# Five edits in a four-layer vision kernel: exp table load, norm shifts, leaky relu, sums of exp, skip loads

## The chip, the cores and the metric

The kernel runs on one core of a Trainium2 chip. The metric is the device time of one execution in microseconds (us). A core has five engines, each with an instruction queue of its own that is worked off in order: TensorE (PE, matmuls; its weight loads are listed as PEld), VectorE (DVE), ScalarE (ACT), GpSimd (POOL) and SyncE (SP, which here only issues DMAs). Engines wait for each other through semaphores.

## The reference

Four layers follow each other on `x[4, 64, 64, 128]` in float32. Layer 0 is a selective scan, layer 1 attention over all 4096 tokens of an image, layer 2 a convolution block, layer 3 attention in a 7 x 7 neighbourhood with an MLP. What the edits touch is this:

```
# layer 0
xn = _ln(input, ln1_w, ln1_b)                       # mean and variance over 128 channels
...
h = exp(d_t[..., None] * A) * h + (d_t * x_t)[..., None] * B_t     # 4096 steps, 4 directions
ys = ... + Ds * xs                                   # the skip term
...
h2 = gelu(_ln(x, ln2_w, ln2_b) @ fc1_w + fc1_b) @ fc2_w + fc2_b
# layer 1
scores = einsum('bnd,bmd->bnm', f, g)
beta = softmax(scores, axis=1)
att = einsum('bnc,bnm->bcm', hv, beta)
# layer 2, end
xc = _bn(concatenate([x1, x2]), bn_cat)
xc = where(xc >= 0, xc, 0.1 * xc)
# layer 3
attention(_ln(x)), then x + mlp(_ln(x)) with gelu
```

## The kernel before

**Stages.** `network` (L1611) first makes the inputs of image 0's scan (`scan_inputs`, L275). Then `selective_scan` (L451) runs for the images 0 to 3, one after the other, and beside each scan the other work of the images is put: beside image 0's scan the scan inputs of images 1 to 3, beside the scan of image i the stages of image i - 1 (`rest`, L1579: `scan_output`, `layer1`, `layer2`, `layer3_attention`). The MLP of layer 3 of an image runs within the `scan_output` of the next one. For image 3 nothing is left to put beside it: its stages run alone at the end with `wide` true (larger tiles, since the scan's buffers are free), and last comes `layer3_mlp_alone`.

**Order.** The order of each engine's queue is laid down when the program is built, by a scheduler that simulates the program's time and takes, of the instructions that are ready, the one with the smallest priority number. The scan is traced with a large number (`SCAN_FIRST`), the activations of a group and the table load after it with a very small one (-100 * `SCAN_FIRST`), the rest in order of tracing. So an edit can also shift instructions around it.

**The scan.** One unit covers 64 of 256 channels, 4 of 16 states and 512 steps: a product `dB` on POOL (L498, 128x1024), two exponentials `dA` on ACT (L504, 128x512 into PSUM, three buffers), two scans on DVE (L506), two products with C (L511 on DVE, or one L519 on POOL for 5 or 7 units of 16), and a copy of the last state on ACT (L513, L515). `total` (L527) adds up with PE (L553) into `py`; with `j == 0` it first loads a tile `y_before` (three buffers) and adds it to `py`: for direction 0 the skip term, read from `xc` in four DMAs of 32 partitions (L535), for directions 2 and 3 the sums of earlier directions (L540, L544). These loads share SP's queue with those of `dt`, `du` (L481) and `bc` (L489).

**Table loads.** ACT has one table of functions active at a time; exp and ln are in one, gelu and silu in others. `Together` (L101) collects the gelu or silu activations of a chunk, makes all of them wait for the group's last matmul, and then calls `exp_table` (L95), which loads the table with exp and ln. That load depends on the group's last activation by a dependency of the kind `Sync`. Where the program has an activation whose function isn't in the active table, a load is put ahead of it when the program is built, and the profile shows it under that activation's line.

**Norms.** `layernorm_T` (L179) takes 4 x 128 tokens: statistics on DVE (L188, L190), rstd on ACT as exp(-0.5 ln(var + eps)) (L175, L176), the shift -mean * rstd for the four tiles on DVE (L192, 128x4), four scaled copies on ACT (L196), four transposes on PE (L199) and one activation (L200). It is called 128 times: 32 chunks each in `scan_tokens`, `scan_output`, `layer3_attention` and `layer3_mlp`.

**Layer 1.** For each of 8 chunks of 512 columns and 8 steps t: four score matmuls (L783), exp on ACT (L787, one instruction of 128x2048 when `wide`), four matmuls with the values into `pa` (L831), and four with ones into `den` (L839), which gives the sums of exp. The scores of step t + 1 are traced ahead of the products of step t. A float32 matmul is two instructions in the profile, so a group of four counts 8.

**Layer 2, end.** For each of 8 chunks (L965): normalisation from PSUM into `t` on ACT (L973), max(0.1 t, t) on DVE (L974), a matmul with `cv4` (L981), and the last activation (L983, L984).

Of the kernel before, what the change touches and what calls it, by code (L numbers as in the profile page):

```python
# [27 lines left out]
F32 = mybir.dt.float32  # L28
AF = mybir.ActivationFunctionType
ALU = mybir.AluOpType  # L30
# [11 lines left out]
LC = 512  # L42
NCH = NT // LC
RC = LC // W
# [27 lines left out]
def span(c, n=LC):  # L72
    return slice(c * n, (c + 1) * n)
# [9 lines left out]
    tc.cur_priority = kept  # L83


def after(tc, later, earlier):
    tc.add_manual_dep(
        later.ins,
        earlier.ins.name,
        mybir.DependencyInfo(mybir.DependencyClass.Sync, mybir.DependencyReason.DATA),  # L90
        reason="group",
    )


def exp_table(tc, K, done):  # L95

    with priority(tc, K, -100 * SCAN_FIRST):
        after(tc, tc.nc.scalar.preload_act_table_set("natural_log_exp_and_others"), done)


class Together:  # L101
# [77 lines left out]
def layernorm_T(tc, K, pool, psum, x, w, b, out):  # L179


    nc = tc.nc
    stats = pool.tile([128, 4, 6], F32, name="ln_stats", bufs=2)
    mv = pool.tile([128, 4, 2], F32, name="ln_mv", bufs=2)
    rstd = pool.tile([128, 4], F32, name="ln_rstd", bufs=2)
    shift = pool.tile([128, 4], F32, name="ln_shift", bufs=2)
    for t in range(4):
        nc.vector.bn_stats(stats[:, t, :], x[:, t, :])  # L188
    for t in range(4):
        nc.vector.bn_aggr(mv[:, t, :], stats[:, t, :])  # L190
    rstd_of(nc, K, rstd, mv[:, :, 1])
    nc.vector.scalar_tensor_tensor(shift, mv[:, :, 0], -1.0, rstd, ALU.mult, ALU.mult)  # L192
    xn = pool.tile([128, 4, 128], F32, name="ln_xn", bufs=1)
    pt = psum.tile([128, 4, 128], F32, name="ps")
    for t in range(4):
        nc.scalar.activation(  # L196
            xn[:, t, :], x[:, t, :], AF.Identity, bias=shift[:, t : t + 1], scale=rstd[:, t : t + 1]
        )
        nc.tensor.transpose(pt[:, t, :], xn[:, t, :], K.ident)  # L199
    nc.scalar.activation(out, pt.rearrange("p t c -> p (t c)"), AF.Identity, bias=b, scale=w)  # L200
# [250 lines left out]
def selective_scan(tc, K, S, D, img):  # L451
# [8 lines left out]
    nc = tc.nc  # L460
    pool, psum = S.pool, S.psum
# [6 lines left out]
    for k in ORDER:  # L468
# [4 lines left out]
        for i in range(NCH):  # L473
            c = NCH - 1 - i if back else i
            for hf in range(2):
                dts, dus = [], []
                for pp in range(2):
                    rows = span(2 * hf + pp, 32)
                    for name, src, out in (("dt", D.delta, dts), ("du", D.du, dus)):
                        t = pool.tile([128, 2, LC], F32, name=name, bufs=4)  # L480
# [6 lines left out]
                for j in range(NJS):  # L487
# [6 lines left out]
                    hcs, made = [], []  # L494
# [32 lines left out]
                    def total(k=k, c=c, hf=hf, j=j, hcs=hcs, made=made, py=py):  # L527
                        if j == 0:
                            py.append(psum.tile([128, LC], F32, name="py"))
                            before = pool.tile([128, LC], F32, name="y_before", bufs=3)  # L530
                            if k == 0:
                                for pp in range(2):
                                    for g in range(2):
                                        q = 2 * pp + g
                                        nc.sync.dma_start(  # L535
                                            before[32 * q : 32 * q + 32, :], D.xc[img][c][span(2 * hf + pp, 32), g, :]
                                        )
                                nc.tensor.matmul(py[0], S.skip[:, hf, :], before, start=True, stop=False)
                            elif k >= 2:
                                nc.sync.dma_start(before, D.y_first[img][k % 2][c][:, hf, :])  # L540
                                nc.tensor.matmul(py[0], K.ident, before, start=True, stop=False)
                            if k == 2:
                                cols = pool.tile([128, NCH, RC, RC], F32, name="y_before", bufs=3)
                                nc.sync.dma_start(  # L544
                                    cols.rearrange("p c a b -> p c (a b)"),
                                    D.y_cols[img][:, :, c, hf].rearrange("c p x -> p c x"),
                                )
                                nc.tensor.matmul(
                                    py[0].rearrange("p (a c b) -> p a c b", a=RC, b=RC), K.ident,
                                    cols.rearrange("p c a b -> p a c b"), start=False, stop=False,  # L550
                                )
                        for q in range(4):
                            mm = nc.tensor.matmul(  # L553
                                py[0][32 * q : 32 * q + 32, :], S.pick, hcs[q // 2][:, q % 2, :],
                                start=(k == 1 and j == 0), stop=(j == NJS - 1),
                            )
                            if q == 0:
                                for m in made:
                                    after(tc, mm, m)
                        if j == NJS - 1:  # L560
                            y = pool.tile([128, LC], F32, name="y_sum")
                            if k == 3:
                                nc.scalar.copy(
                                    y.rearrange("p (b a) -> p b a", b=H), py[0].rearrange("p (a b) -> p b a", b=H)
                                )
                                nc.scalar.dma_start(
                                    D.y_cols[img][c][:, :, hf, :], y.rearrange("p (r x) -> p r x", r=NCH)
                                )
                            else:
                                nc.scalar.copy(y, py[0])  # L570
                                to = D.y[img][c] if k == 2 else D.y_first[img][k % 2][c]
                                nc.scalar.dma_start(to[:, hf, :], y)
# [145 lines left out]
def layer1(tc, K, A, D, img, xT, wide):  # L718
# [4 lines left out]
    nc = tc.nc  # L723
    NP = 4 if wide else 2
    with ExitStack() as ctx:
        big = ctx.enter_context(tc.tile_pool(name="l1_big", bufs=1))
        pool = ctx.enter_context(tc.tile_pool(name="l1", bufs=1))
        psum = ctx.enter_context(tc.tile_pool(name="l1_p", bufs=1, space=PSUM))
        load = loader(tc, big, A, 1)
# [47 lines left out]
        def scores(c, t):  # L777
            es = []
            for p in range(4 // NP):
                ps = pair(NP)  # L780
                for u in range(NP):
                    quad = span(NP * p + u, 32)
                    nc.tensor.matmul(  # L783
                        ps[:, u, :], f[quad, t // 4, span(t % 4, 128)], g[quad, c, :], start=True, stop=True
                    )
                e = pool.tile([128, NP, LC], F32, name="e", bufs=10 // NP)
                made = nc.scalar.activation(e, ps, AF.Exp)  # L787
                es += [e[:, u, :] for u in range(NP)]
            return es, made

        xT_view = xT.rearrange("c (p j) -> c j p", j=NJ)

# [29 lines left out]
        for c in range(NCH):  # L822
            pa = psum.tile([128, LC], F32, name="pa")
            den = None
            ready = scores(c, 0)
            for t in range(8):
                es, made = ready
                if t + 1 < 8:
                    ready = scores(c, t + 1)
                for q in range(4):  # L830
                    nc.tensor.matmul(  # L831
                        pa, v[:, 8 * q + t, :], es[q],
                        start=(t == 0 and q == 0), stop=(t == 7 and q == 3),
                    )
                if not K.general:
                    if den is None:
                        den = psum.tile([128, LC], F32, name="den")
                    for q in range(4):
                        mm = nc.tensor.matmul(  # L839
                            den[32 * q : 32 * q + 32, :], K.ones[:, :32], es[q],  # L840
                            start=(t == 0), stop=(t == 7),
                        )
                        if q == 0:
                            after(tc, mm, made)
                if c == 0 and t in (1, 3, 5) and not K.general:
                    keys((t + 1) // 2)
            finish(c, pa, den)
# [55 lines left out]
def layer2(tc, K, A, D, img, xT, wide):  # L903
# [3 lines left out]
    nc = tc.nc  # L907
    with ExitStack() as ctx:
        big = ctx.enter_context(tc.tile_pool(name="l2_big", bufs=1))
        pool = ctx.enter_context(tc.tile_pool(name="l2_w", bufs=2))  # L910
        psum = ctx.enter_context(tc.tile_pool(name="l2_ps", bufs=8 if wide else 4, space=PSUM))
        load = loader(tc, big, A, 2)
# [5 lines left out]
        norms = load("norms", [128, len(NORMS2), 4], D.w2_norms)  # L918
# [46 lines left out]
        for c in range(NCH):  # L965
# [5 lines left out]
            nc.tensor.matmul(ps[64:128, :], cv2p, xT[:, span(c)], start=True, stop=True)  # L971
            t = pool.tile([128, LC], F32, name="cat")
            nc.scalar.activation(t, ps, AF.Identity, bias=norms[:, 5, 1:2], scale=norms[:, 5, 0:1])  # L973
            nc.vector.scalar_tensor_tensor(t, t, 0.1, t, ALU.mult, ALU.max)  # L974
            po = psum.tile([128, 4, 128], F32, name="ps")
            nc.tensor.matmul(
                po.rearrange("p t c -> p (t c)"), K.ones[0:1, :], bias.rearrange("p t c -> p (t c)"),
# [768 lines left out]
```

## Time and profile before

| what | value |
|---|---|
| median of three runs | 9356.33 us (9351.10 to 9378.78) |
| profiled execution: time, span | 9352.68 us, 9350.9 us |
| instructions | 99598 |
| PE busy | 7472.2 us, 80% of the span |
| DVE busy | 7109.1 us, 76% |
| POOL busy | 7052.9 us, 75% |
| ACT busy | 5607.1 us, 60% |
| mean granted PE clock | 0.85 |

The page names a group of instructions by its line, engine and operation, then the tiles that it writes and reads with their shapes, the count, the busy time in us and the mean of one in ns, and after a second bar the time that the engine sat idle just before them and what ended it. In a list of waits a row reads "engine, line that waited <- what it waited for: us in total, times, longest". In a timeline a row begins with the start and the duration in us. In the page's second part each digit is the busy share of one fortieth of the span, in tenths.

### The profile page before, as it was taken

To read this page: it belongs to the slowest core of one execution; us is meant where nothing else is said; L and a number is where in the kernel's file an instruction comes from. 1 tells how busy PE (TensorE), PEld (TensorE's weight loads), DVE (VectorE), ACT (ScalarE), POOL (GpSimd) and SP (SyncE) were. 2 spreads that over 40 slices of the span, in tenths; PEclk is the share of its full clock that TensorE was granted. 3 is DMA by queue.
4 is the path that set the end of the run, shared out by engine and by line. 5 is a ranking of instruction groups with operands and counts; after the bars stand their busy time and mean duration, and the time that the engine had idled before them with its cause. 6 is when DMAs were issued, how large, how long until landed. Compare 5 with 4: busy or idle time off the path is not lost. (4 is left out here: it accounts for less than half of the span.)

```text
span 9350.9 us, 99598 instructions
## 1 busy us (share of the span) xinstructions
PE 7472.2 (80%) x30564; PEld 2808.5 (30%) x30564; DVE 7109.1 (76%) x8543; ACT 5607.1 (60%) x10676; POOL 7052.9 (75%) x3064
## 2 busy tenths in 40 slices
PE   8647768696779997787789988877799977788987
PEld 3112222231332232233322333333222322343333
DVE  0798787777889988988899989888999898820033
ACT  4646666665566666557766655567666555553345
POOL 1977988979789988987899979987999699800000
PEclk9658678686789998888899988888899888889988
DMA  2766766667544546565455555554455455510020
GB/s 101 262 216 214 250 216 222 248 208 271 183 154 169 176 155 210 175 209 173 142 173 178 178 180 178 190 196 151 160 179 175 152 198 176 196 40 3 1 82 28
DMA packets 720492, 1581.76 MB, mean 169 GB/s; under 512 B 207157, under 2 KB 332236, under 8 KB 715597
## 3 DMA queue, kind: packets, MB, share of 16 engines
q1 hardware_dynamic: 589645, 1399.12, 44.1%
q10 hardware_dynamic: 130304, 176.19, 5.3%
q8 instruction: 245, 4.01, 0.2%
q14 instruction: 298, 2.44, 0.1%
HBM read 1280.47 MB, written 283.59 MB: 167 GB/s over the span
## 5 line engine op out<-in xcount | busy, mean ns | idle before, releaser
L498 POOL TENSOR_TENSOR dB<-du,bc 128x1024 f32<-128x1024 f32 x2048 | 4806.9, 2378 | 699.3 <-DVE hc L506 229.0
L504 ACT ACTIVATE dA<-dt,w_A_log 128x512 f32<-128x512 f32 x4096 | 2782.1, 689 | 569.5 <-DVE hc L506 284.3
L506 DVE TENSOR_TENSOR_SCAN dA<-dA,state,dB 128x512 f32<-128x512 f32 x2128 | 2627.0, 1272 | 382.5 <-POOL dB L498 187.8
L519 POOL TENSOR_TENSOR hc<-hc,bc 128x1024 f32<-128x1024 f32 x832 | 1976.3, 2380 | 238.8 <-ACT state L515 131.1
L506 DVE TENSOR_TENSOR_SCAN hc<-dA,state,dB 128x512 f32<-128x512 f32 x1456 | 1800.6, 1267 | 279.4 <-ACT dA L504 133.8
L511 DVE TENSOR_TENSOR hc<-dA,bc 128x512 f32<-128x512 f32 x2432 | 1560.5, 675 | 91.7 <-PE py L553 82.4
L553 PE MATMUL py<-hc,pick 128*32 128x512 f32 x8192 | 1276.3, 699 | 316.7 <-POOL hc L519 208.3
L513 ACT COPY state<-dA 128x1 f32<-128x1 f32 x2128 | 327.7, 158 | 1349.5 <-DVE hc L511 1328.5
L831 PE MATMUL pa<-e,l_v 128*128 128x512 f32 x2048 | 1062.9, 649 | 5.1 <-ACT e L787 3.9
L787 ACT ACTIVATE e<-pair 128x1024 f32<-128x1024 f32 (+1 forms) x448 | 508.0, 1134 | 271.3 <-PE pair L783 268.6
L783 PE MATMUL pair<-l_g,l_f 32*128 32x512 f32 x2048 | 530.7, 668 | 168.1 <-ACT e L787 125.9
L831 PEld LDWEIGHTS pa<-e,l_v 128*128 128x128 f32 x2048 | 371.9, 199 | 661.6 <-issue 637.8
L553 PEld LDWEIGHTS py<-hc,pick 128*32 128x32 f32 x8192 | 217.2, 118 | 1093.0 <-issue 500.4
L1272 PE MATMUL pair<-table,ident 128*128 128x512 f32 x768 | 420.8, 674 | 115.1 <-ACT e L1282 90.9
L506 DVE TENSOR_TENSOR_SCAN dA<-dA,dB 128x512 f32<-128x512 f32 x304 | 357.7, 1212 | 200.2 <-POOL dB L498 166.5
L245 PE MATMUL ps<-band,w_conv_diag 128*128 128x504 f32 (+3 forms) x1152 | 493.1, 586 | 4.1 <-ACT band L314 3.4
L408 PE MATMUL ps<-xdbl,w_dt_w 9*128 9x512 f32 x512 | 351.0, 935 | 181.0 <-ACT delta L359 128.1
L416 POOL TENSOR_TENSOR du<-delta,xc 128x1024 f32<-128x1024 f32 x128 | 337.1, 2639 | 177.0 <-DMA bc_dram<-xdbl 160.5
L199 PE MATMUL ps<-ident,ln_xn 128*128 128x128 f32 x512 | 132.3, 356 | 356.3 <-ACT ln_xn L196 287.2
L1282 ACT ACTIVATE e<-pair 128x1024 f32<-128x1024 f32 (+1 forms) x224 | 254.2, 1135 | 153.4 <-PE pair L1276 153.0
L217 PE MATMUL ps<-xnT,w_fc_w 128*128 128x512 f32 x512 | 275.6, 672 | 66.8 <-ACT mlp_h L224 27.3
L231 PE MATMUL ps<-mlp_h,w_fc_w 128*128 128x512 f32 x512 | 283.5, 702 | 53.9 <-ACT mlp_h L224 53.9
(270 smaller groups left out, 8547.6 us busy)
## 6 DMA issues: line engine op xcount, KB each, us to landing
bc<-bc_dram SPq DMA_DIRECT2D x1024, 512.0 KB
dt<-delta_dram SPq DMA_DIRECT2D x512, 512.0 KB
du<-du_dram SPq DMA_DIRECT2D x512, 512.0 KB
delta_dram<-delta ACTq DMA_DIRECT2D x128, 512.0 KB
du_dram<-du SPq DMA_DIRECT2D x128, 512.0 KB
table<-biasT_dram SPq DMA_DIRECT2D x72, 512.0 KB
y_first_dram<-y_sum ACTq DMA_DIRECT2D x128, 256.0 KB
y_before<-y_first_dram SPq DMA_DIRECT2D x128, 256.0 KB
```

The source lines that it names most:

```text
L245: mm = nc.tensor.matmul(out[:, r0 - row0 : r1 - row0, c0:c1], lhsT((dy + 1) * 3 + dx + 1), src[:, r0 + dy : r1 + dy, c0 + dx : c1 + dx], s ...
L408: nc.tensor.matmul(pd[:, d, :], dt_w[rows, o, d * 128 : (d + 1) * 128], xdbl[rows, i, :], start=True, stop=True,)
L498: nc.gpsimd.tensor_mul(dB, dus[pp], mid(bct[:, 0, :], 2))
L504: nc.scalar.activation(dA, dts[pp][:, g, :], AF.Exp, scale=S.A[:, k, j, pr, g : g + 1])
L506: nc.vector.tensor_tensor_scan(hg[:, order], dA[:, order], dB[:, g, order], 0.0 if i == 0 else state[:, j, pr, g : g + 1], ALU.mult, ALU.add,)
L511: mm = nc.vector.tensor_mul(hc[:, g, :], dA, bct[:, 1, :])
L519: made.append(nc.gpsimd.tensor_mul(hc, hc, mid(bct[:, 1, :], 2)))
L553: mm = nc.tensor.matmul(py[0][32 * q : 32 * q + 32, :], S.pick, hcs[q // 2][:, q % 2, :], start=(k == 1 and j == 0), stop=(j == NJS - 1),)
L783: nc.tensor.matmul(ps[:, u, :], f[quad, t // 4, span(t % 4, 128)], g[quad, c, :], start=True, stop=True)
L787: made = nc.scalar.activation(e, ps, AF.Exp)
L831: nc.tensor.matmul(pa, v[:, 8 * q + t, :], es[q], start=(t == 0 and q == 0), stop=(t == 7 and q == 3),)
L1272: nc.tensor.matmul(ps[:, u, :], K.ident, t[:, u, :], start=True, stop=False)
```

## The change

1. `after` takes a kind of dependency, and the exp table's load now hangs on the group's last activation by `NoSync`: the order stays, without a semaphore between them.
2. `layernorm_T` makes the shift on ACT: -rstd once for the four tiles (`less`), then four activations of one column each, mean times `less`. The instruction L192 on DVE is gone.
3. `y_before` has four buffers in place of three, and the skip term is loaded in two DMAs of 64 partitions in place of four of 32.
4. In `wide` layer 1 (image 3 only), DVE adds the tiles of exp over the eight steps of a chunk in `total` (a copy at t = 0, adds after), and only at t = 7 four matmuls with ones make `den` of it.
5. At the end of layer 2 a second activation writes the normalised value into PSUM in place, and the maximum on DVE reads it there, in place of reading `t` twice.

```diff
-def after(tc, later, earlier):
+def after(tc, later, earlier, kind=mybir.DependencyClass.Sync):
     tc.add_manual_dep(
-        later.ins,
-        earlier.ins.name,
-        mybir.DependencyInfo(mybir.DependencyClass.Sync, mybir.DependencyReason.DATA),
-        reason="group",
+        later.ins, earlier.ins.name, mybir.DependencyInfo(kind, mybir.DependencyReason.DATA), reason="group"
     )
...
     with priority(tc, K, -100 * SCAN_FIRST):
-        after(tc, tc.nc.scalar.preload_act_table_set("natural_log_exp_and_others"), done)
+        load = tc.nc.scalar.preload_act_table_set("natural_log_exp_and_others")
+        after(tc, load, done, mybir.DependencyClass.NoSync)
...
+    less = pool.tile([128, 4], F32, name="ln_less", bufs=2)
     shift = pool.tile([128, 4], F32, name="ln_shift", bufs=2)
...
-    nc.vector.scalar_tensor_tensor(shift, mv[:, :, 0], -1.0, rstd, ALU.mult, ALU.mult)
+    nc.scalar.activation(less, rstd, AF.Copy, scale=-1.0)
+    for t in range(4):
+        nc.scalar.activation(shift[:, t : t + 1], mv[:, t, 0:1], AF.Copy, scale=less[:, t : t + 1])
...
-                            before = pool.tile([128, LC], F32, name="y_before", bufs=3)
+                            before = pool.tile([128, LC], F32, name="y_before", bufs=4)
                             if k == 0:
                                 for pp in range(2):
-                                    for g in range(2):
-                                        q = 2 * pp + g
-                                        nc.sync.dma_start(
-                                            before[32 * q : 32 * q + 32, :], D.xc[img][c][span(2 * hf + pp, 32), g, :]
-                                        )
+                                    nc.sync.dma_start(
+                                        before[span(pp, 64), :],
+                                        D.xc[img][c][span(2 * hf + pp, 32)].rearrange("d g t -> g d t"),
+                                    )
...
-                                cols = pool.tile([128, NCH, RC, RC], F32, name="y_before", bufs=3)
+                                cols = pool.tile([128, NCH, RC, RC], F32, name="y_before", bufs=4)
...
-            return es, made
+            return es, made, e
...
-                es, made = ready
+                es, made, e4 = ready
...
-                if not K.general:
+                if wide:
+                    if t == 0:
+                        total = pool.tile([128, NP, LC], F32, name="total", bufs=2)
+                        nc.vector.tensor_copy(total, e4)
+                    else:
+                        nc.vector.tensor_add(total, total, e4)
+                    if t == 7:
+                        es, made = [total[:, q, :] for q in range(4)], None
+                if not K.general and (t == 7 or not wide):
                     if den is None:
                         den = psum.tile([128, LC], F32, name="den")
                     for q in range(4):
                         mm = nc.tensor.matmul(
                             den[32 * q : 32 * q + 32, :], K.ones[:, :32], es[q],
-                            start=(t == 0), stop=(t == 7),
+                            start=(t == 0 or wide), stop=(t == 7),
                         )
-                        if q == 0:
+                        if q == 0 and made is not None:
                             after(tc, mm, made)
...
-            nc.vector.scalar_tensor_tensor(t, t, 0.1, t, ALU.mult, ALU.max)
+            nc.scalar.activation(ps, ps, AF.Identity, bias=norms[:, 5, 1:2], scale=norms[:, 5, 0:1])
+            nc.vector.scalar_tensor_tensor(t, t, 0.1, ps, ALU.mult, ALU.max)
```

## The prediction

> **What bounds the kernel now.** I read the page's slices first, then the waits of the stretch in which the scan runs (222 to 8205 us), then the rows of the edited lines, then timelines.
>
> ```profile
> PE   8647768696779997787789988877799977788987
> DVE  0798787777889988988899989888999898820033
> ACT  4646666665566666557766655567666555553345
> POOL 1977988979789988987899979987999699800000
> ```
>
> One digit is 233.8 us. GpSimd (POOL) and VectorE (DVE) are at eight or nine tenths until slice 35; then POOL has nothing left and PE carries the last 1146 us alone. So there are two regimes, and each edit is priced in the one it falls in. In the scan's 7983 us POOL is busy 7016.1, DVE 6888.7, ScalarE (ACT) 5001.4. POOL's work is untouched by the diff, so only its 967 us of idle time can shrink. What ended that idle time:
>
> ```profile
> POOL dB L498 <- DVE hc L506: 229.0, 72, 21.4
> POOL dB L498 <- DMA bc<-bc_dram: 200.0, 86, 11.5
> POOL hc L519 <- ACT state L515: 131.1, 61, 6.5
> POOL dB L498 <- DVE dA L506: 101.4, 39, 7.5
> POOL hc L519 <- DVE hc L506: 78.4, 25, 13.7
> ```
>
> (us in total, times, longest.) Three of these five rows are DVE: 408.8 us. It lies where norms run beside the scan: from 4200 to 4600 us POOL is busy 313.5 of 400, while from 7000 to 7200 it has no gap at all.
>
> ```profile
> L192 DVE SCALAR_TENSOR_TENSOR ln_shift<-ln_mv,ln_rstd 128x4 f32<-128x4 f32 x128 | 113.1, 894 | 71.9 <-ACT ln_rstd L176 71.4 <-ACT state L513 0.3
> L974 DVE SCALAR_TENSOR_TENSOR cat<-cat 128x512 f32<-128x512 f32 x32 | 38.0, 1187 | 9.9 <-ACT cat L973 9.9
> L98 ACT ACT_TABLE_LOAD x100 | 128.3, 1283 | 1.8
> L504 ACT ACT_TABLE_LOAD x44 | 56.5, 1283 | 0.8
> ```
>
> The norm's shift has four elements per partition and a mean of 894 ns. Its median is 164 ns and its longest 7483; after 8205 us, with POOL silent, 27 of them take 4.05 us (150 ns each). Something holds it while POOL works. The last row is the other oddity: an activation of the scan reloads the table 44 times, although L98 reloads it 100 times on purpose. A timeline of ACT shows why:
>
> ```profile
> 9257.26 2.42 ACT L224 ACTIVATE mlp_h<-ps,w_fc_b 128x512 f32<-128x512 f32 x4 [0.95 <-PE ps L217]
> 9259.70 1.28 ACT L175 ACT_TABLE_LOAD   x1
> 9261.00 0.30 ACT L175 ACTIVATE ln_rstd<-ln_mv,eps 128x4 f32<-128x4 f32 x1
> 9261.31 1.28 ACT L98 ACT_TABLE_LOAD   x1
> ```
>
> The planned load (L98) had been put behind another activation, which needed the same table and got a load of its own; the planned one then loads it a second time. L504 (44), L175 (12) and L176 (2) hold 58 such loads, 50 of them within the scan.
>
> Last, the last image's attention, PE alone:
>
> ```profile
> 8576.99 3.70 PE L831 MATMUL pa<-e,l_v 128*128 128x512 f32 x8
> 8580.62 1.07 PE L839 MATMUL den<-e,ones 128*32 128x512 f32 x8
> 8581.61 1.14 PE L783 MATMUL pair<-l_g,l_f 32*128 32x512 f32 x8
> 8582.68 3.70 PE L831 MATMUL pa<-e,l_v 128*128 128x512 f32 x8
> ```
>
> A step t lasts 5.69 us with no gap on PE: values 3.63, sums of exp 0.99, next scores 1.07 (start to start).
>
> **What the Trainium skill says.** "SBUF — State Buffer", section "SBUF: two separate sides": DVE and GpSimd share a port pair under an exclusive lock; a DVE instruction with two SBUF inputs waits for a whole GpSimd instruction that reads SBUF. The trace agrees: L192 and L974 have two SBUF inputs and stretch beside POOL; L984, same size as L974 with one PSUM input, has a mean of 671 ns. "ScalarE: Activation LUTs", section "What ACT_TABLE_LOAD costs": 1283 ns for a load, which every row here has, plus a drain of 1380, which this trace does not show (after the load at 9259.70 the next activation starts 0.02 us later). It also prices an activation at 186 ns + 0.833 per element + 93 per pointer operand, with 93 of overlap back to back; L196 (128 elements, two pointers) should be 479 and has a median of 482. "VectorE: DVE Perf Modes", its perf-mode tier table: an fp32 add of 2048 takes 2293 ns (L1284 here: 2292), an fp32 copy 1227.
>
> **Part 1, sums of exp on DVE (last image).** Of 8 x 8 groups of den matmuls, 7 x 8 = 56 go, 0.99 us each: **-55.6 us**, all of it on PE, which sets the end there. Added: per chunk one copy (1.23 us by the skill) and seven adds (2.29 us by L1284). The cover is the shortened step of 4.70 us; DVE is busy only 17.2 of 400 us between 8500 and 8900. The last add is ready 2.3 us after the last exp; den is asked for after another 3.63 us of values, so PE doesn't wait. If the adds took over 4.70 us the step would follow DVE. The e buffer (two) is released later by the add, but its next use is 4.7 us on. Behind an add in DVE's queue can stand the maximum L748, three times in the first chunk, for which PE already waits 3.9 us in all; up to 2.3 us each, I take +2. Sum **-54**.
>
> **Part 2, norm shift to ACT.** 128 norms. Removed from DVE: within the scan 93 instructions and 107.8 us (26.1 + 16.2 + 28.1 + 37.4 by stretch), DVE's head-of-queue wait for rstd there (15.4 us), and ACT's wait for the shift (79.2 us: 9.1, 15.8, 19.9, 34.4). Added to ACT per norm: five instructions. Floor: three one-element copies run in 0.26 us in this trace, so 0.45; ceiling: five times L175's 0.29 without overlap, 1.45. By the skill's formula 0.19 + 4 x 0.28 - 3 x 0.09 = 1.03 us, which I take: 96 us within the scan. Behind them in ACT's queue stand the scan's dA, for which DVE waits (363 us today).
>
> **Part 3, table load.** If each planned load directly follows its group, the 58 doubles go: 58 x 1.283 = 74.4 us of ACT, 64.2 within the scan. Removing the wait itself is worth nothing: 1.8 us idle before all 100. Bounds: 0 (the order stays) to 74.4; I take all of it as ACT time.
>
> **Part 4, leaky relu.** DVE within the scan: 24 x (1.352 - 0.671) = 16.3 us less. ACT: one more activation from PSUM with two pointers, 0.777 us by L973: 24 x 0.777 = 18.6 us within the scan. In the last image layer 2 is bound by PE (110.6 of 120 us), so eight more cost at most the last one, 0.8.
>
> **Part 5, skip term.** 128 issues fewer on SP at a median of 0.41 us: 53 us of a queue that mostly waits for buffers (1108 and 1064 us for bc buffers alone). Same bytes, same rows. The fourth y_before buffer lets these loads be queued earlier. Bounds: a gain up to part of the 200 us in which POOL waits for bc; a loss as in rival D. I take 0.
>
> **Sum.** Within the scan DVE gets back 107.8 + 15.4 + 16.3 = 139.5 us; ACT 64.2 + 79.2 - 96 - 18.6 = 29 us. What of that reaches the end? POOL waits for DVE in a share of the time only; where norms run, POOL stands for about 22% and DVE is at 85%, so DVE sets the pace there about half the time. I take 0.45 of 139.5 (63) and little of ACT's (2): **-65**, bounds 0 and -168. In the last 1146 us: five iterations of the last MLP lose a double load on the chain (5 x 1.28 = 6.4), but rstd's successor now has 1.03 us of shift on the same engine ahead of yT, leaving about 3; the other norms there can lie on the chain with 0.6 more each, some six of them: +4. Total -54 - 65 - 3 + 4 = -118. Against the profiled execution (span 9350.9, time 9352.7) that gives 9234.7; the median shown, 9356.3, is 3.6 higher: **9238**.
>
> **Rivals.**
> - A (0.50), as summed: 9238, own range 9190 to 9285.
> - B (0.20), POOL's rhythm absorbs what DVE gains, because POOL's fixed 7016 us and its bc waits decide: only the last stretch counts, 9356 - 53 = 9303. For it: POOL is at 88% of the scan. Against it: 409 us of its idle time ends with DVE.
> - C (0.15), everything freed arrives: 9356 - 53 - 168 = 9135. For it: chained waits between three in-order engines can multiply a stall. Against: clean stretches where DVE has slack.
> - E (0.09), the load keeps its place behind other work: 64 us of ACT stay, the added 115 us count at about 0.3 more, +20: 9258.
> - D (0.06), slower: in SP's in-order queue a y_before load that is ready one buffer earlier waits at the head for a matmul to free it (891 us of such waits today) and the bc loads behind it land late. Today bc costs POOL 200 us in 86 waits, 2.3 each; from 118 us more (3.7 each) it eats the whole gain, and at 4.2 each the time is about 9400.
>
> **Numbers.** Range 9145 to 9310: it takes in A and E, most of B and the upper part of C. About 0.3% (28 us) is what a measurement can tell from no change: faster 0.88 (A, C, E and nearly all of B), the same 0.06 (B or E with a dearer last stretch), slower 0.06 (D).
>
> **What would show it.** Right: steps of 4.7 us in the last attention and den groups down by 56; no table load at L504, L175 or L176; no DVE row for the shift; POOL's waits for DVE down from 409 by 60 or more; the scan's end near 8140 instead of 8205. Wrong: DVE adds longer than a step, POOL's bc waits above 300 us, or DVE's waits for dA above 363 us (the shift on ACT delaying the scan).

## The result, and the profile after

The changed kernel takes 9242.15 us (median of four runs, 9231.94 to 9246.99), the kernel before 9359.24 beside it: ratio 0.987, 95% interval 0.9853 to 0.9888. Forecast was 9238. The profiled execution took 9231.94 us (span 9230.1), the one before 9352.68 (9350.9), at granted clocks of 0.852 and 0.850.

The page's slices, one digit for 230.8 us:

```profile
PE   7647768697678998887689987877799888877987
DVE  0698777777899988988899979988899889812433
ACT  4655666666566666666766666667666666554355
POOL 1977988979889988997799979988899889900000
```

The two regimes are still there: POOL and DVE mostly at seven to nine tenths to slice 35, then PE alone. DVE's last four digits, 0033 before, are 2433: the sums of exp. To see where the time went, I cut both traces at the same events (us; first product `dB`, end of the last scan, first and last matmul with the values of image 3's layer 1, last add after the attention of layer 3):

| stretch | before | after | difference |
|---|---|---|---|
| start to first dB | 239.1 | 255.2 | +16.1 |
| first dB to end of the last scan | 7962.1 | 7823.9 | -138.2 |
| end of the scan to image 3's layer 1 | 288.2 | 352.3 | +64.1 |
| layer 1 of image 3 | 404.9 | 343.4 | -61.5 |
| layer 2 and attention | 333.9 | 342.0 | +8.1 |
| last MLP | 122.7 | 113.2 | -9.5 |
| span | 9350.9 | 9230.1 | -120.8 |

The second and third row belong together. Here is the first `scan_output` matmul of image 3 in PE's timeline, in the kernel before and then in the changed one:

```profile
8128.66 5.19 PE L613 MATMUL ps<-y,center 128*128 128x512 f32 x8 [1.96 <-ACT dA L504]
```

```profile
8087.28 4.90 PE L613 MATMUL ps<-y,center 128*128 128x512 f32 x6 [4.77 <-DMA y<-y_dram]
```

Before, it starts 72.5 us ahead of the scan's end (8201.2); after, 8.1 us behind it (8079.1). The scan came forward by 122 us on the clock, the work beside it by only 41. So image 3's `scan_output` lost the overlap that it had, and from the first dB to layer 1 the gain is 74 us, not 138.

POOL's waits for other engines in the changed kernel (us in total, times, longest):

```profile
POOL dB L499 <- DMA bc<-bc_dram: 170.9, 83, 10.4
POOL dB L499 <- DVE hc L507: 160.6, 63, 25.8
POOL dB L499 <- DVE dA L507: 149.9, 43, 21.0
...
POOL hc L520 <- ACT state L516: 92.3, 44, 9.6
...
POOL hc L520 <- DVE hc L507: 36.6, 21, 9.2
```

The three rows with DVE are 347.1 us, where they were 408.8. The rows of the edited lines (busy time in us, mean in ns, then idle time before them):

```profile
L840 DVE TENSOR_TENSOR total<-total,e 128x2048 f32<-128x2048 f32 x56 | 128.4, 2293 | 122.9 <-ACT e L787 122.9
L95 ACT ACT_TABLE_LOAD x100 | 128.3, 1283 | 1.8
L193 ACT ACTIVATE ln_shift<-ln_mv,ln_less 128x1 f32<-128x1 f32 x512 | 107.6, 283 | 1.5
...
L191 ACT ACTIVATE ln_less<-ln_rstd 128x4 f32<-128x4 f32 x128 | 24.5, 201 | 2.3 <-ACT ln_rstd L174 0.7
...
L983 DVE SCALAR_TENSOR_TENSOR cat<-cat,ps 128x512 f32<-128x512 f32 x32 | 21.8, 682 | 14.1 <-ACT ps L982 14.1
```

An add costs 2293 ns, the shift 132.1 us of ACT for 128 norms (1.03 each), and the maximum fell from 1187 to 682 ns. L95 still has its 100 loads, but the loads under the lines of the scan's exp and of rstd (44 + 12 + 2) are down to 3. ACT's timeline shows it in the last MLP:

```profile
9147.47 2.42 ACT L225 ACTIVATE mlp_h<-ps,w_fc_b 128x512 f32<-128x512 f32 x4 [0.95 <-PE ps L218]
9149.92 1.28 ACT L95 ACT_TABLE_LOAD   x1
9151.21 0.30 ACT L173 ACTIVATE ln_rstd<-ln_mv,eps 128x4 f32<-128x4 f32 x1
9151.54 0.21 ACT L174 ACTIVATE ln_rstd<-ln_rstd 128x4 f32<-128x4 f32 x1
```

The planned load now stands directly behind its group, and one serves where two were. And PE's timeline of the last image's layer 1:

```profile
8641.13 1.14 PE L783 MATMUL pair<-l_g,l_f 32*128 32x512 f32 x8
8642.20 3.70 PE L831 MATMUL pa<-e,l_v 128*128 128x512 f32 x8
8645.83 1.14 PE L783 MATMUL pair<-l_g,l_f 32*128 32x512 f32 x8
```

The step is 4.70 us, with no `den` group in it.

### The profile page after: what moved, and what is told of

Read it like the earlier page. It is cut to its first block, busy times and chain, and to the rows that moved or that the text cites. A ratio compares the mean times of both kernels' runs of the same rounds, so it can differ in the third digit from the quotient of the medians.

```text
span 9230.1 us, 99135 instructions
## 1 busy us (share of the span) xinstructions
PE 7385.0 (80%) x30116; PEld 2800.0 (30%) x30116; DVE 7119.9 (77%) x8479; ACT 5664.3 (61%) x11293; POOL 7049.3 (76%) x3064
## 5 line engine op out<-in xcount | busy, mean ns | idle before, releaser
L499 POOL TENSOR_TENSOR dB<-du,bc 128x1024 f32<-128x1024 f32 x2048 | 4791.2, 2362 | 639.1 <-DMA bc<-bc_dram 170.9
L246 PEld LDWEIGHTS ps<-band,w_conv_diag 128*128 128x128 f32 x1152 | 217.3, 190 | 279.1 <-issue 257.8
```

Source lines behind the costliest of these rows:

```text
L246: mm = nc.tensor.matmul(out[:, r0 - row0 : r1 - row0, c0:c1], lhsT((dy + 1) * 3 + dx + 1), src[:, r0 + dy : r1 + dy, c0 + dx : c1 + dx], s ...
L499: nc.gpsimd.tensor_mul(dB, dus[pp], mid(bct[:, 0, :], 2))
```

## The experiments

Unless said otherwise, each variant is made from the kernel before. Ratios are to the kernel before, run on the same chip. Stage lengths are from one profiled execution each. They have a limit: where an edit does not touch the scan at all (the sums of exp alone), its profiled scan was still 38 us longer than the one before, so differences of 20 to 40 us in a single scan are not evidence by themselves. Other stages vary too: image 3's layer 1 takes 401.0 to 405.0 us in the nine kernels that keep its old form, and its layer 2 with the attention 333.9 to 341.8 in four kernels that leave these stages alone (before, sums of exp, both skip variants).

### The five parts alone

Sums of exp only:

```diff
...
+                if wide:
+                    if t == 0:
...
+                        nc.vector.tensor_copy(total, e4)
+                    else:
+                        nc.vector.tensor_add(total, total, e4)
...
-                if not K.general:
+                if not K.general and (t == 7 or not wide):
...
```

> Before, with the sums of exp on VectorE in the last image as the only edit. Theory (each part is worth its own term of the sum): 54 us less than before, ratio 0.994, all of it in the last image's layer 1, whose steps fall from 5.7 to 4.7 us; the scan does not move. Rival (the order of the whole program shifts with any edit): the scan's length moves by 20 us or more although nothing in it was edited.

Measured: 9306.88 us, ratio 0.9933 (0.9921 to 0.9946). Layer 1 of image 3 went from 404.9 to 343.4 us, to the tenth what it has in the full change. Over all kernels the stage takes 401.0 to 405.0 us without this edit and 343.4 to 346.2 with it, so the edit is worth 55 to 62 us there, and it stands by itself: the whole kernel is 62 us faster.

Norm shifts only:

```diff
-    nc.vector.scalar_tensor_tensor(shift, mv[:, :, 0], -1.0, rstd, ALU.mult, ALU.mult)
...
+    nc.scalar.activation(less, rstd, AF.Copy, scale=-1.0)
+    for t in range(4):
+        nc.scalar.activation(shift[:, t : t + 1], mv[:, t, 0:1], AF.Copy, scale=less[:, t : t + 1])
```

> Before, with the norm shift on ScalarE as the only edit. Theory: VectorE gets back some 108 us of held instructions within the scan and ScalarE's wait for the shift goes; at 0.45 that is 50 us off, ratio 0.995. Rival (GpSimd's own rhythm absorbs it): within 10 us of before. Rival (the five activations per norm delay the scan's exponentials): slower than before.

Measured: 9340.45 us, ratio 0.9969 (0.9957 to 0.9981). The scan took 7857.8 us, 104 less, nearly all of the 123 us that DVE gets back. But image 3's first `scan_output` matmul moved only from 8129 to 8109, the scan's end to layer 1 grew from 288 to 356, and the last MLP from 122.7 to 131.8. Scan and background work are two streams: this edit speeds up the first, and over two thirds of that is lost where the second has to be waited for (104 us of scan, 28 of the kernel).

Table load only:

```diff
...
-        after(tc, tc.nc.scalar.preload_act_table_set("natural_log_exp_and_others"), done)
+        load = tc.nc.scalar.preload_act_table_set("natural_log_exp_and_others")
+        after(tc, load, done, mybir.DependencyClass.NoSync)
```

> Before, with the exp table's load tied by order alone as the only edit. Theory: the 58 double loads go (74 us of ScalarE time), of which some 15 us arrive at the end, 6 of them in the last MLP; ratio 0.998. Rival (ScalarE's stalls are what holds the scan beside the norms): 40 us or more off. Rival (the load keeps its place): double loads stay and the time is that of before.

Measured: 9335.72 us, ratio 0.9965 (0.9954 to 0.9975). It is the mirror image: the scan's length hardly moved (7951.0), but `scan_output` of image 3 began at 8092 instead of 8129, the scan's end to layer 1 fell to 266.8, and the last MLP to 110.2. The first dB came 12.9 us later.

Leaky relu only:

```diff
-            nc.vector.scalar_tensor_tensor(t, t, 0.1, t, ALU.mult, ALU.max)
+            nc.scalar.activation(ps, ps, AF.Identity, bias=norms[:, 5, 1:2], scale=norms[:, 5, 0:1])
+            nc.vector.scalar_tensor_tensor(t, t, 0.1, ps, ALU.mult, ALU.max)
```

> Before, with the leaky relu reading PSUM as the only edit. Theory: VectorE gets back 16 us within the scan, of which some 7 arrive, too little to measure; L974 falls from a mean of 1187 ns to about 670. Rival (order shifts with any edit): a change of 20 us or more either way.

Measured: 9358.89 us, ratio 0.999 (0.9983 to 0.9996), some 9 us.

Skip term only (two loads and the fourth buffer):

```diff
-                            before = pool.tile([128, LC], F32, name="y_before", bufs=3)
+                            before = pool.tile([128, LC], F32, name="y_before", bufs=4)
...
-                                    for g in range(2):
-                                        q = 2 * pp + g
-                                        nc.sync.dma_start(
-                                            before[32 * q : 32 * q + 32, :], D.xc[img][c][span(2 * hf + pp, 32), g, :]
-                                        )
+                                    nc.sync.dma_start(
+                                        before[span(pp, 64), :],
+                                        D.xc[img][c][span(2 * hf + pp, 32)].rearrange("d g t -> g d t"),
+                                    )
...
```

> Before, with the skip term's two loads and the fourth y_before buffer as the only edit. Theory: 0; SP issues 128 loads fewer, and nothing waits for them; GpSimd's waits for bc stay near 200 us. Rival (loads queued earlier stand before the bc loads): GpSimd's waits for bc above 250 us and the time 30 us or more up. Rival (SP's queue holds the scan): 30 us or more off.

Measured: 9427.92 us against 9365.0, ratio 1.0068 (1.0052 to 1.0083). This part alone makes the kernel slower, by 63 us. The product of the other four ratios is 0.9858, of all five 0.9925; the full change has 0.987. So the parts do not multiply: in the full change most of this loss is not seen.

### The skip loads without the fourth buffer

```diff
-                                    for g in range(2):
...
+                                    nc.sync.dma_start(
+                                        before[span(pp, 64), :],
+                                        D.xc[img][c][span(2 * hf + pp, 32)].rearrange("d g t -> g d t"),
+                                    )
```

> Before, with the skip term in two loads of 64 partitions, and still three y_before buffers. The two edits of part 5 together gave 63 us more, three quarters of it while direction 0 of the scan runs. Theory (the loads themselves do it): 40 to 60 us more than before. Rival (the fourth buffer does it, by loads that stand earlier in SP's queue): within 15 us of before.

Measured: 9424.04 us, ratio 1.0057 (1.0044 to 1.0069). With three buffers the loss is nearly the same; it is the loads themselves. Where it is lost, single profiles don't settle. Only direction 0 has these loads, and there the scan falls back by 12.8, 31.7, 7.6 and -9.1 us in the four images, 43 together; but with the table load alone, whose loads are the old ones, it falls back by 38 in the same places. At its end the scan is only 32 us late, while image 3's `scan_output` begins 111 us later (8239.5). What differs for certain is how the loads are carried. The page's line on DMA packets, before and then here:

```profile
DMA packets 720492, 1581.76 MB, mean 169 GB/s; under 512 B 207157, under 2 KB 332236, under 8 KB 715597
```

```profile
DMA packets 716653, 1581.75 MB, mean 168 GB/s; under 512 B 203318, under 2 KB 328397, under 8 KB 711758
```

The bytes are the same, and 3839 packets are missing, all under 512 B; by size in the trace they are 3840 packets of 4 bytes, 30 for each of the 128 new loads. The Trainium skill ("DMA: Bandwidth & Descriptors", section "Why a DMA increments its semaphore by 16 and not by 1") says that each participating DMA engine ends its part with an increment of the semaphore, and that the number of engines is the largest up to 16 that divides the slowest dimension of both patterns. The old loads have 32 rows there, so 16 engines and 16 increments, twice: 32. The new one has the two `g` in front, so two engines and two increments: 30 fewer, as counted. (The semaphore's own record has 16 updates for each old load and three for each new one; the page says that the sequencer adds what the engines leave of the 16.) The time from issue to the last increment follows (us, from the completion records of the trace, 1200 to 8000 us):

| load | before: median, 90% | skip loads: median, 90% |
|---|---|---|
| `y_before` from `xc` | 2.46, 5.10 | 7.69, 11.23 |
| `bc` | 5.17, 7.24 | 5.26, 7.88 |
| `dt` | 4.53, 6.58 | 4.67, 7.69 |
| `du` | 5.55, 7.38 | 5.70, 8.20 |

A skip load takes three times as long on two engines, and the transfers that share these two have a longer tail. POOL waits 236.7 us for `bc` where it waited 200.0. That two engines carry the new load is what the count and the page say together; that the longer landings are the cause of the 55 us is argued: POOL's row has 37 of them, and the edit also shifts the order of the queues. A pattern of 64 partitions that spreads over all engines, which would separate the two, was not tried.

### What held the shift: one operand in PSUM

```diff
-    nc.vector.scalar_tensor_tensor(shift, mv[:, :, 0], -1.0, rstd, ALU.mult, ALU.mult)
...
+    nc.scalar.copy(pt[:, 0, 0:4], rstd)
+    nc.vector.scalar_tensor_tensor(shift, mv[:, :, 0], -1.0, pt[:, 0, 0:4], ALU.mult, ALU.mult)
```

> Before, with the norm shift still on VectorE, but rstd read from a copy in PSUM (one more small copy on ScalarE), so that the instruction has one SBUF input. Theory (the shared port holds it): its mean falls from 894 ns to under 250, VectorE is busy about 85 us less in the scan, ScalarE's wait for the shift stays by half or more; some 20 to 30 us off, most of what the shift on ScalarE alone gave (29). Rival (it is held by its place in the queue or by its operands' arrival): its mean stays above 500 ns and the time is that of before.

Measured: 9325.90 us, ratio 0.9956 (0.9941 to 0.9971). The rows:

```profile
L193 ACT COPY ps<-ln_rstd 128x4 f32<-128x4 f32 x128 | 21.1, 169 | 11.6 <-DVE x L642 5.4 <-DVE T L1186 3.6 <-DVE x L1562 1.5
L194 DVE SCALAR_TENSOR_TENSOR ln_shift<-ln_mv,ps 128x4 f32<-128x4 f32 x128 | 18.8, 151 | 276.9 <-ACT ps L193 276.9
```

The same operation on DVE, with one of its two inputs from PSUM, has a mean of 151 ns where it had 894, and none of the 128 takes more than 163 ns. This shows that the second SBUF input was what held it, as the Trainium skill has it ("SBUF — State Buffer", section "SBUF: two separate sides"). The longest one in the kernel before shows more, beside POOL's timeline:

```profile
7729.07 4.63 POOL L498 TENSOR_TENSOR dB<-du,bc 128x1024 f32<-128x1024 f32 x2
7733.67 2.33 POOL L519 TENSOR_TENSOR hc<-hc,bc 128x1024 f32<-128x1024 f32 x1
7735.96 2.33 POOL L498 TENSOR_TENSOR dB<-du,bc 128x1024 f32<-128x1024 f32 x1
```

```profile
7730.83 7.48 DVE L192 SCALAR_TENSOR_TENSOR ln_shift<-ln_mv,ln_rstd 128x4 f32<-128x4 f32 x1
```

It begins within one product and ends 0.02 us after the third one behind that: it waited not for one whole GpSimd instruction, as the prediction took from the page, but until an unbroken row of them was over (8 of the 128 take longer than one product, 2378 ns on average). In the variant, DVE idles 276.9 us for the copy instead, and still the kernel is about as fast as with five activations on ACT (0.9956 and 0.9969, with intervals that overlap).

### The shift a second time

```diff
     nc.vector.scalar_tensor_tensor(shift, mv[:, :, 0], -1.0, rstd, ALU.mult, ALU.mult)
...
+    nc.vector.scalar_tensor_tensor(again, mv[:, :, 0], -1.0, rstd, ALU.mult, ALU.mult)
```

The second result is not used.

> Before, with the norm shift computed twice on VectorE (the second result is not used). Theory (VectorE's time beside the norms reaches the scan's end nearly whole, as the 94 to 116 us show by which the last product of the scan came earlier without it): the second one waits less than the first, being next to it, some 0.2 to 1 us each; the scan ends 20 to 100 us later and the time is 20 to 80 us up, in step with L192's busy time. Rival (the gain of the shift edit came from another order of the queues): the time is within 15 us of before.

Measured: 9383.95 us against 9367.47, ratio 1.0019 (1.001 to 1.0028). The rows:

```profile
L192 DVE SCALAR_TENSOR_TENSOR ln_shift<-ln_mv,ln_rstd 128x4 f32<-128x4 f32 x128 | 100.1, 783 | 81.1 <-ACT ln_rstd L176 78.8 <-ACT state L515 2.2
L194 DVE SCALAR_TENSOR_TENSOR ln_again<-ln_mv,ln_rstd 128x4 f32<-128x4 f32 x128 | 28.2, 221 | 0.0
```

The second, right behind the first, takes 221 ns: it does not wait again. So doubling the instruction did not double the cost; DVE got 15.2 us more, the kernel 17 us more. But the theory's way there did not show: in the profiled execution the scan is no longer than before (7959.2 us, ended at 8202.0), and it is image 3's `scan_output` that begins later, at 8169.8 instead of 8128.7. So this run does not say that time of DVE lengthens the scan one for one, and an effect of 17 us is too near the rival's 15 to refute another order of the queues.

### A second table load behind each planned one

Made from the variant with the table load only; each group is followed by a load of another table and then by the planned one.

```diff
+        other = tc.nc.scalar.preload_act_table_set("gelu_and_others")
+        after(tc, other, done, mybir.DependencyClass.NoSync)
         load = tc.nc.scalar.preload_act_table_set("natural_log_exp_and_others")
-        after(tc, load, done, mybir.DependencyClass.NoSync)
+        after(tc, load, other, mybir.DependencyClass.NoSync)
```

> The exp table's load tied by order alone, and ahead of each of the 100 one more load of another table: 128 us of ScalarE time on top, 88 of them within the scan. Theory (what the table edit gave is ScalarE's time, about half of which reaches the end in the scan): 44 us for the scan, 11 at the start, 10 in the last MLP, so 60 to 70 us over the kernel with the table edit alone. Rival (that gain came from another order of the queues): within 20 us of it.

Measured: 9491.9 us, ratio 1.0134 (1.0119 to 1.015), some 156 us more than with the table load only, more than twice what the theory gave. The loads are as meant:

```profile
L98 ACT ACT_TABLE_LOAD x100 | 128.3, 1283 | 1.8
L100 ACT ACT_TABLE_LOAD x100 | 128.3, 1283 | 0.5
```

128.3 us of ACT cost 156. The scan's end did not move for it (8205.4, against 8203.0), but image 3's `scan_output` began at 8264 instead of 8092, here with the table load only and then with the second load:

```profile
8091.95 5.23 PE L614 MATMUL ps<-y,center 128*128 128x512 f32 x8 [9.88 <-DMA w_fc_w<-in_L_conv_fc_w]
```

```profile
8264.22 5.77 PE L616 MATMUL ps<-y,center 128*128 128x512 f32 x8 [13.64 <-DMA y<-y_dram]
```

The background stream takes all of it: its groups (matmuls, gelu or silu, table, next norm) are a chain, and a load behind each group lies on that chain. This is the clearest sight of the two streams.

### The full change with the old forms at both ends

In image 0's scan inputs, and in all of image 3's stages after the scan, the shift is the old one on DVE; in image 0's scan inputs, the load depends by `Sync`. The rest is the changed kernel.

```diff
-        after(tc, load, done, mybir.DependencyClass.NoSync)
+        after(tc, load, done, mybir.DependencyClass.Sync if K.first_image else mybir.DependencyClass.NoSync)
...
+    if K.alone:
+        nc.vector.scalar_tensor_tensor(shift, mv[:, :, 0], -1.0, rstd, ALU.mult, ALU.mult)
+    else:
...
```

> The changed kernel, except where GpSimd does nothing: for image 0's scan inputs and for image 3's own stages the shift is on VectorE again, and for image 0's scan inputs the table load hangs on its group by Sync. Theory: the start falls back from 255 to about 240 us, the last image's norms lose some 0.7 us each on their chain; 15 to 25 us less than the changed kernel. Rival: those 16 us of the start and the tail's norms are hidden, and the time is that of the changed kernel.

Measured: 9206.89 us, ratio 0.9828 (0.9814 to 0.9841), some 35 us under the changed kernel and more than the theory's 15 to 25. First dB at 241.7 instead of 255.2, the scan's end where it was (8077.4), the scan's end to layer 1 337.5 (352.3), layer 2 and attention 337.6 (342.0), the last MLP 110.0 (113.2). So the old forms at the start bring the scan forward by 13.5 us; by the parts alone, the table load had delayed it by 12.9 and the shift by 3.7. But the scan then ends no earlier, and what this trace gains shows behind it, most of it before layer 1. The two ends were not reverted one at a time. That loads which come at once there stand ahead of copies and norms that the first scan waits for is how the start's timelines look; it was not tested by itself.

### The same without the new skip loads

```diff
-                            before = pool.tile([128, LC], F32, name="y_before", bufs=4)
+                            before = pool.tile([128, LC], F32, name="y_before", bufs=3)
...
-                                        D.xc[img][c][span(2 * hf + pp, 32)].rearrange("d g t -> g d t"),
...
+                                            before[32 * q : 32 * q + 32, :], D.xc[img][c][span(2 * hf + pp, 32), g, :]
```

> The kernel with the edits kept off the ends (after_ends), without part 5: three buffers and four loads as before. Theory (part 5 costs some 63 us wherever it stands): 9150. Rival (part 5's cost depends on the order around it, and the four other parts multiplied give 0.9858 against 0.987 measured for all five): 9180 to 9200, some 10 to 25 us under after_ends.

Measured: 9199.85 us, ratio 0.9808 (0.9792 to 0.9824). The rival came nearer: 9199.85 lies just inside its 9180 to 9200, though the step is under its 10 to 25 us. Taking the loads back gives 7 us or about 0.2% here, with intervals that overlap, not the 0.68% that they cost alone. A skip load lands as late in the full change as alone (median 7.52 us), so the landing is not what differs; POOL waits 170.9 us for `bc` there, 223.2 with the skip part alone. Why the rest of the order covers it in one kernel and not in the other stays open.

### The last version with the shift's operand in PSUM

```diff
...
-        nc.scalar.activation(less, rstd, AF.Copy, scale=-1.0)
-        for t in range(4):
-            nc.scalar.activation(shift[:, t : t + 1], mv[:, t, 0:1], AF.Copy, scale=less[:, t : t + 1])
+        nc.scalar.copy(pt[:, 0, 0:4], rstd)
+        nc.vector.scalar_tensor_tensor(shift, mv[:, :, 0], -1.0, pt[:, 0, 0:4], ALU.mult, ALU.mult)
```

> The version with the old forms at both ends and the four 32-partition loads (9199.85 us), but within the scan the shift is one instruction on VectorE that reads the mean from SBUF and a copy of rstd that ScalarE has put into PSUM, in place of five activations on ScalarE. The copy form alone measured 9326 against 9340 for the five activations alone, both in the kernel before. Theory (the two savings add: ScalarE is relieved of four small activations per norm, VectorE's operation takes 151 ns instead of waiting for the shared port): the same 10 to 15 us again, so 9183 to 9193. Rival (with the table loads cheaper, VectorE's head-of-queue wait for the copy, 277 us in all in the copy form alone, decides, since the scan is VectorE's): no better, 9195 to 9225. Separating figures: the time VectorE waits for the copy in the scan (theory under 277 us), and the scan's end, which was 8058 us in the version without the copy.

Measured: 9187.0 us (9167.25 to 9208.3), ratio 0.981 (0.9794 to 0.9827). The median lies in the theory's figures, and so do its signs in the profile: DVE waits 23.9 us for the copy (88 norms), not 277 (128 norms), and the scan ends at 8027.7 instead of 8057.8. But the ratio is that of the version before it. The two cannot be told apart; a scan that ends 30 us earlier again gives part of it back behind it (scan's end to layer 1: 364.0, from 348.6).

## Why the prediction was right

The time came out 4 us from the forecast, and the directions of likeliest case A held: DVE's freed time shortens the scan, the sums of exp shorten the end. But that it is so near is partly luck, because terms that were off cancel.

One comparison over all fourteen traces shows where the sum's path was wrong. It adds what the scan gains to the kernel's gain. But the time from image 3's first `scan_output` matmul to the end is 1195 to 1240 us in the nine kernels without the sums of exp and 1120 to 1158 in the five with them, while in the nine the time behind the scan's end varies from 1129 to 1268. So the kernel's time follows the start of that stage more closely than the end of the scan. And the stage starts where the background stream lets it: in both traces 17 us behind image 2's last projection on PE (8111.43 and 8070.77). Of the profiled 120.8 us, 41.4 are its earlier start and 79.4 lie behind it, 61.5 of these in layer 1.

- **Sums of exp, -54: right.** Measured -61.5 between these two traces, 55 to 62 over all kernels. A step fell from 5.69 to 4.70 us, so 56 groups give 55.4, as forecast; the rest is within the spread of layer 1. No add was longer than a step (2293 ns against 4.70 us), and PE's wait for `bounds` in layer 1 is unchanged (3.9 us).
- **Scan, -65: the right stages, the wrong sizes.** The step that failed is "I take 0.45 of 139.5". The scan itself gained 138.2, about the whole of the 139.5. The shift alone gave 104 for 123 us of DVE. These are single profiles with a spread of some 40 us, but in the other four kernels without the old shift in the scan (the operand in PSUM alone, and the last three versions) it is 125 to 177 us shorter as well. So the scan's own length took up most of DVE's time, as in rival C; the run with the shift doubled, where 15 us were added, is too small to show the reverse. POOL's share of idle time is no measure of it: its waits for DVE fell by only 62 us, just over the 60 named as a sign, and the row with `dA` even rose (101.4 to 149.9), while the scan gained 138.
- **What the sum left out: +64 behind the scan.** No term of the forecast asked what the scan's end would meet. 72 us of image 3's `scan_output` had lain beside the end of the scan; that overlap is gone, since the background stream came forward by only 41 us. So -138 became -74, near the -65, for another reason. The sign "scan's end near 8140" failed (8079).
- **Shift on ACT, price 1.03 us per norm: right** (1.03). The doubt, that it would delay the scan's exp, did not come true: DVE's waits for `dA` are 340 us (363 before).
- **Table load, 58 doubles: 55 of them went, but "little of ACT's (2)" is wrong.** Alone this part gives 0.35%, some 33 us. ACT's time in table loads is worth little to the scan, as forecast, and much to the background chain, which the forecast did not price: 128 us more of it cost 156. Rival E, that the load keeps its place behind other work, is refuted by the timeline.
- **Leaky relu: right.** A maximum takes 682 ns (671 was taken), its ACT price 743 (777), and alone the part is worth some 9 us.
- **Skip term, 0: wrong.** The reason given was "Same bytes, same rows". The rows are the same but two DMA engines carry them instead of 16, which the diff's `rearrange` tells. Alone it costs 63 us. It was not rival D, whose wait for `bc` had to rise by 118 us: with the part alone it rose by 23. Beside the other parts, taking it back gave 0.2%, which is within the noise.
- **Ends: +4 for norms and -3 for the last MLP.** Layer 2 and attention +8.1, which is no more than the spread of that stage; last MLP -9.5; the start's +16.1 was in no term. The last MLP's two halves show in the parts alone: -12.5 with the table load, +9.1 with the shift.

Rival B fell: the scan did not absorb it. Rival C had the scan right and the rest not: what was freed came out of the scan and was half lost behind it, 64 of 138 us.

## What to carry to other kernels

When two streams of work run beside each other, ask of every saving which of the two it speeds up, and what waits where they meet: the faster stream's gain ends where it has to wait for the other. A busy share below one is no discount for a saving: here DVE's time came out of the scan's length nearly whole (104 of 123 us for the shift), though only 28 us reached the kernel's end, and ACT's time on the background chain cost more than itself (156 for 128). Joining small DMAs into larger ones is not free: look at the outermost dimension of the pattern, which by the page named above sets over how many DMA engines the transfer is spread.

## What the runs showed of the hardware

A DMA of 128 KB whose outermost dimension is 2 has two increments from DMA engines in the trace and lands 7.7 us after its issue (median), while those of 64 KB with 32 rows in front have 16 each and land after 2.5. A DVE operation of four elements per partition with two SBUF inputs had a mean of 894 ns beside GpSimd, 151 ns with one of them in PSUM, and 221 ns right behind another of its kind; one of them took 7483 ns, until a row of GpSimd products without a gap had ended. No drain was seen after a table load: the next activation started 0.01 us after the load at 9149.92 ended.
